# A graph network's hand-over between two layers: four small DMAs against one over 128 partitions

## The chip, the cores and the metric

The kernel runs on one core of one Trainium2 chip. The core has a matrix engine (TensorE, called PE in the profile, with its weight loads as PEld), three engines for elementwise work (VectorE or DVE, ScalarE or ACT, GpSimd or POOL) and a SyncE (SP), which in this kernel only issues transfers. Transfers (DMAs) are issued from SP or from POOL; each engine's instructions and issues start in the order in which they were written. The metric is the device time of one execution in microseconds (us); less is better.

## The reference

The input is a batch of 128 graphs of 128 nodes with 256 features, in float32. Two layers, each a residual step on the normalized input:

```python
# layer 0: all 128 nodes of every graph
h = jnp.maximum(_layernorm(x, axis=-1), 0.0)
x = x + _L0_gnn_ref(h, adj, ...)     # 1x1 and 17-tap convolution, neighbour sums, GRU-like gates
# layer 1: only the nodes in GROUPS, all of them below 25
GROUPS = [list(range(25)), [0, 1, 2, 3, 4, 5, 6, 7, 8], [0, 9, 10, 11, 12, 13, 14],
          [6, 7, 8, 12, 13, 14], [3, 4, 5, 9, 10, 11]]
h = jnp.maximum(_layernorm(x, axis=-1), 0.0)
x = x + _L1_gnn_ref(h, adj, ...)     # five small graph convolutions per graph, fused by weights
return x
```

Layer 1 reads and changes rows 0 to 24 of each graph alone. So rows 32 to 127 are final when layer 0 is done, and the first 32 rows have to be handed over from layer 0 to layer 1.

## The kernel before

Layer 0 works on *groups* of `GB = 4` graphs, 32 groups in all. Its convolution has a first pass (`stage_a`, four batches of 8 groups) and a middle pass per batch (`stage_b`, products in the frequency domain). The neighbour sums and gates follow group by group in `stage_n` and `stage_c`. Layer 1 works on *blocks* of `SB = 16` graphs, that is `QS = 4` groups, 8 blocks in all, in two steps: `prepare` (adjacency, row statistics) and `block` (the convolutions).

Every stage is a Python generator that emits instructions and yields an estimated cost. A small planner (`Order`, `Lane`) takes turns between the generators by those costs and their due times. What it emits is the fixed order of instructions on each engine; at run time the engines only wait for each other through semaphores. Until the last `stage_b` has ended, `stage_n` and `stage_c` run beside `stage_a` and `stage_b`; after it (about 1355 us into the span) they run beside layer 1.

At the end of `stage_c` a group's result stands in the tile `xt`, 128 partitions by 4 rows of 256: partition `32 j + n` holds rows `n`, `n + 32`, `n + 64` and `n + 96` of the group's graph `j` (`WIDE = 32`). `xt` was loaded with the residual input by `load_x` (L358, four DMAs on SP), and L832 (DVE) adds the layer's result. There is one `xt` buffer, so SP's next `load_x` into it waits until all stores out of it have landed, and what stands behind it on SP waits too: the filter weights `wf` (L488), inputs `xa` (L358), the layer's inputs `hT` (L540, L640) and `yt` (L562), and in layer 1 `aj` (L929) and the weights `w` (L897).

The stores are issued from POOL, graph by graph: L838 stores the graph's first 32 rows (`xt[:, 0]`) to a scratch buffer in DRAM, `x1d`, one per block, and L839 stores the other 96 rows to `out`. For the last four groups the block tile of layer 1 exists already; L829 adds straight into it and L838 is left out. POOL's other work, in whose queue the stores stand, is the reciprocal root of the row statistics (L278), the sums `xs` and `wf` of `stage_b` (L496, L497), the gate blend of `stage_c` (L810 to L813), the stores of `hTd`, `yd` and `xmd`, and in layer 1 `b` (L936), `dm` (L962 to L964), `x1h` (L913) and the stores of the finished blocks (L1077).

In layer 1 `load_x1` (L919, on SP, called in `prepare` or `rows_of_x`) fetches a block's hand-over from `x1d` into a tile of 128 partitions by 4 groups by 256. It has two buffers, so it waits for the stores L1077 of the block before the last. `rows_of_x` then computes the row statistics (L275, DVE) and the normalized rows `x1h`. In the trace the block tile is called `x`.

Of the kernel before, what the change touches and what calls it, by code (L numbers as in the profile page):

```python
# [20 lines left out]
GB = 4  # L21
# [10 lines left out]
SB = 16  # L32
QS = SB // GB
# [9 lines left out]
WIDE = 32  # L43
# [165 lines left out]
def kernel(ctx: ExitStack, tc: tile.TileContext, x, adj, consts, vecs, w_se, conv1_w,  # L209
                    conv2_w, w_msg, b_msg, w_ih, w_hh, W1, W2, b2, fusion_w, out):  # L210
    nc = tc.nc
# [15 lines left out]
    x1d = [dr.tile([SB, WIDE, D], FP, name=f"x1d{b}") for b in range(NBLK)]  # L227
# [308 lines left out]
    IN, IN2, X1, N_DONE = {}, {}, {}, set()  # L536
# [119 lines left out]
    def stage_c(q):  # L656
# [108 lines left out]
        xt = LATE["io"].tile([P, 4, D], FP, tag="xt", name=f"xt{q}", bufs=1)  # L765
# [54 lines left out]
        direct = X1.get(q // QS)  # L820
        for h in range(2):
            po = ptmp.tile([P, 2, D], FP, tag="tmp", name=f"po{q}_{h}")
            for i in range(2):
                t = 2 * h + i
# [6 lines left out]
            else:  # L831
                nc.vector.tensor_add(xt[:, 2 * h:2 * h + 2], xt[:, 2 * h:2 * h + 2], po)  # L832
        yield 0.9, 1.5
        for j in range(GB):
            rows = xt[j * WIDE:(j + 1) * WIDE]
            g = q * GB + j
            if direct is None:
                nc.gpsimd.dma_start(out=x1d[g // SB][g % SB], in_=rows[:, 0])  # L838
            nc.gpsimd.dma_start(out=out[g, WIDE:].rearrange("(t n) c -> n t c", n=WIDE),  # L839
                                in_=rows[:, 1:4])  # L840
        C_DONE.add(q)


# [55 lines left out]
    def rows_of_x(blk, wait=True):  # L899

        ready = all(q in C_DONE for q in range(blk * QS, (blk + 1) * QS))
        if blk in S or not (wait or ready and blk - 1 in Y_DONE):
            return
        while not (all(q in C_DONE for q in range(blk * QS, (blk + 1) * QS))
                   and blk - 1 in Y_DONE):
            yield 0.0, 0.5
        if blk not in X1:
            load_x1(blk)
            yield 0.0, 6.0
        pool2 = S["pool2"]  # L910
        x1h = S[blk] = pool2.tile([P, QS, D], FP, tag="x1h", name=f"x1h{blk}", bufs=1)
        normalize(x1h, X1[blk], *moments(X1[blk], "b"))
        nc.gpsimd.tensor_scalar(x1h, x1h, 0.0, None, op0=ALU.max)  # L913
        yield 0.0, 8.0 if wait else 0.0

    def load_x1(blk):
        X1[blk] = S["pool2"].tile([P, QS, D], FP, tag="x1", name=f"x1_{blk}")
        for j in range(GB):
            nc.sync.dma_start(out=X1[blk][j * WIDE:(j + 1) * WIDE],  # L919
                              in_=x1d[blk].rearrange("(q j) n c -> j n q c", j=GB)[j])  # L920

    def prepare(blk):

# [7 lines left out]
        if blk not in X1 and all(q in C_DONE for q in range(blk * QS, (blk + 1) * QS)):  # L931
            load_x1(blk)
# [164 lines left out]
    for blk in range(NBLK):  # L1097
        second += [prepare(blk), block(blk)]
    groups = Lane([stage(q) for q in range(NQ) for stage in (stage_n, stage_c)], ahead=2)
    side = Lane(first, weight=0.5)  # L1100
    order.run(groups, side, until=side)
# [42 lines left out]
```

## Time and profile before

| | us |
|---|---|
| median of 5 runs | 2212.25 (2208.79 to 2215.77) |
| the profiled execution, its own time | 2210.70 |
| its span, first to last instruction | 2208.92 |
| TensorE busy | 2126.2 (96%) |
| VectorE busy | 1161.9 (53%) |
| GpSimd busy | 793.8 (36%) |
| ScalarE busy | 730.4 (33%) |
| 112 stores to `x1d` (L838), time on POOL | 58.4 |
| 128 stores to `out` (L839), time on POOL | 72.0 |
| SP waiting at `load_x` for stores to `out` | 228.6 |

The profile is one execution. A group's line gives the program line, engine, operation, tiles and count. A wait's line reads: who waited (engine, tile, line), for whom, then the total in us, the number of times, and the longest. A DMA's line gives destination and source, the issuing queue, the count, the KB of each and the median time from issue to landing in us. In a timeline a line begins with the start in us and the duration. `PEclk` is the clock that TensorE was granted, as a share of full speed. POOL's DMA issues count as busy time of POOL, SP's do not. Idle time of an engine that is not the bound costs nothing.

### The profile page before, as it was taken

To read this page: it belongs to the slowest core of one execution; us is meant where nothing else is said; L and a number is where in the kernel's file an instruction comes from. 1 tells how busy PE (TensorE), PEld (TensorE's weight loads), DVE (VectorE), ACT (ScalarE), POOL (GpSimd) and SP (SyncE) were. 2 spreads that over 40 slices of the span, in tenths; PEclk is the share of its full clock that TensorE was granted. 3 is DMA by queue.
4 is the path that set the end of the run, shared out by engine and by line. 5 is a ranking of instruction groups with operands and counts; after the bars stand their busy time and mean duration, and the time that the engine had idled before them with its cause. 6 is when DMAs were issued, how large, how long until landed. Compare 5 with 4: busy or idle time off the path is not lost.

```text
span 2208.9 us, 30690 instructions
## 1 busy us (share of the span) xinstructions
PE 2126.2 (96%) x11308; PEld 1676.6 (76%) x11308; DVE 1161.9 (53%) x2659; ACT 730.4 (33%) x1519; POOL 793.8 (36%) x978
## 2 busy tenths in 40 slices
PE   6999899999999999999999999899999999999997
PEld 3578778888878888888788887677777877767765
DVE  4565446645457654446554545554554554454442
ACT  2432233322234432234443332234334333332332
POOL 2227513265523245542225554232223323213320
PEclk9899999999999999999999999999999999999999
DMA  9888624454533354443335444122223223222221
GB/s 182 226 257 266 224 77 128 121 177 148 158 95 99 93 153 148 148 124 87 97 97 155 146 141 140 39 77 69 76 67 87 67 58 87 65 56 61 88 70 48
DMA packets 193976, 259.64 MB, mean 118 GB/s; under 512 B 21981, under 2 KB 157154, under 8 KB 192290
## 3 DMA queue, kind: packets, MB, share of 16 engines
q1 hardware_dynamic: 165682, 175.89, 28.0%
q0 software_dynamic: 27312, 81.03, 12.1%
q8 instruction: 90, 1.47, 0.3%
q10 hardware_dynamic: 832, 0.75, 0.2%
q14 instruction: 60, 0.49, 0.1%
HBM read 178.44 MB, written 79.17 MB: 117 GB/s over the span
## 4 chain that ended last, share of the span: by engine, by line
PE 83%; DVE 8%; DMA 4%; ACT 2%; POOL 2%; issue 1%; SPq 0%; DVEq 0%; POOLq 0%; ACTq 0%
PE p L710 32%; PE pa L502 7%; PE pg L774 5%; PE pc L396 4%; PE pm L592 4%; PE ph L1015 4%; PE pz L1024 4%; PE pb L502 3%; PE pf L409 3%; PE px L617 2%; PE pi L675 2%; PE pc L689 1%; PE ph L383 1%; PE pg L1057 1%; DMA hTd<-hTa 1%
## 5 line engine op out<-in xcount | busy, mean ns | idle before, releaser
L502 PE MATMUL pa<-wf,X 128*128 128x256 f32 x768 | 182.0, 380 | 0.6 <-DMA wf<-wfd 0.6
L278 POOL TENSOR_TENSOR rs<-rs,cst 128x4 f32<-128x4 f32 x40 | 41.4, 1034 | 363.6 <-DVE rs L277 349.8
L502 PEld LDWEIGHTS pa<-wf,X 128*128 128x128 f32 x768 | 144.7, 190 | 23.3 <-issue 3.0
L810 POOL TENSOR_TENSOR d<-hT,r 128x512 f32<-128x512 f32 x64 | 81.9, 1280 | 218.0 <-ACT r L807 218.0
L525 DVE SCALAR_TENSOR_TENSOR y<-pa,kk 128x512 f32<-128x512 f32 x92 | 63.6, 691 | 154.8 <-ACT kk L524 147.4
L496 POOL TENSOR_TENSOR xs<-X 128x256 f32<-128x256 f32 x92 | 68.6, 746 | 190.0 <-PE pb L502 166.8
L710 PE MATMUL p<-th,wrz 128*128 128x256 f32 x512 | 133.9, 384 | 0.0
L710 PE MATMUL p<-tc,wrz 128*128 128x256 f32 x512 | 131.7, 380 | 2.1 <-DVE tc L552 2.1
L710 PE MATMUL p<-tm,wrz 128*128 128x256 f32 x512 | 131.7, 380 | 0.0
L396 PE MATMUL pc<-c1w,hTa 128*128 128x256 f32 x512 | 127.8, 395 | 2.2 <-ACT hTa L385 2.2
L396 PEld LDWEIGHTS pc<-c1w,hTa 128*128 128x128 f32 x512 | 98.4, 196 | 33.0 <-issue 10.3
L592 PE MATMUL pm<-wmsg,hT 128*128 128x256 f32 x512 | 122.7, 384 | 0.0
L774 PE MATMUL pg<-hT,whn 128*128 128x512 f32 x256 | 122.2, 603 | 0.0
L497 POOL TENSOR_TENSOR wf<-wf 128x512 f32<-128x512 f32 x92 | 116.6, 1268 | 11.1 <-DMA wf<-wfd 11.1
L592 PEld LDWEIGHTS pm<-wmsg,hT 128*128 128x128 f32 x512 | 97.0, 192 | 24.4 <-issue 11.3
L1015 PE MATMUL ph<-yz,w 128*128 128x96 f32 (+3 forms) x640 | 111.7, 329 | 2.8 <-DVE yz L1000 1.9
L524 ACT ACTIVATE kk<-pb 128x256 f32<-128x256 f32 x92 | 35.3, 384 | 230.2 <-PE pb L502 230.2
L1017 ACT ACTIVATE hh<-ph,vec 128x96 f32<-128x96 f32 (+3 forms) x160 | 62.7, 402 | 141.6 <-PE ph L1015 134.2
L710 PEld LDWEIGHTS p<-tc,wrz 128*128 128x128 f32 x512 | 96.8, 190 | 16.6 <-DVE tc L552 3.4
L1024 PE MATMUL pz<-hh,w 128*128 128x96 f32 (+3 forms) x640 | 108.1, 323 | 1.3 <-DVE aT L609 1.3
L710 PEld LDWEIGHTS p<-th,wrz 128*128 128x128 f32 x512 | 95.6, 191 | 16.7 <-issue 3.8
L1015 PEld LDWEIGHTS ph<-yz,w 128*128 128x128 f32 x640 | 89.3, 196 | 24.5 <-issue 14.4
(205 smaller groups left out, 4644.6 us busy)
## 6 DMA issues: line engine op xcount, KB each, us to landing
wf<-wfd SPq DMA_DIRECT2D x192, 256.0 KB, 3.2
yd<-y POOLq DMA_DIRECT2D x96, 256.0 KB, 2.5
yt<-yd SPq DMA_DIRECT2D x64, 384.0 KB, 4.2
hT<-hTd SPq DMA_DIRECT2D x40, 512.0 KB, 6.4
w<-in_W SPq DMA_DIRECT2D x40, 512.0 KB, 3.8
xa<-in_x SPq DMA_DIRECT2D x128, 128.0 KB, 4.9
hTd<-hTa POOLq DMA_DIRECT2D x32, 512.0 KB, 4.5
xt<-in_x SPq DMA_DIRECT2D x128, 128.0 KB, 2.8
```

Of the source, the lines that this page charges most:

```text
L396: nc.tensor.matmul(pc[:, i], hT[:, k, (2 * h + i) * N:(2 * h + i + 1) * N], c1w[:, k], start=(k == 0), stop=(k == 1))
L409: nc.tensor.matmul(pf[:, i, :F * NB], h1[:, 2 * h + i, k * P:(k + 1) * P], fwd, start=True, stop=True)
L496: nc.gpsimd.tensor_tensor(XS[f], X[:, :, 2 * f], X[:, :, 2 * f + 1], ALU.add)
L497: nc.gpsimd.tensor_tensor(WF[f][:, :, 2], WF[f][:, :, 0], WF[f][:, :, 1], ALU.add)
L502: nc.tensor.matmul(ps, xk(k), WF[f][:, k, s], start=(k == 0), stop=(k == 1))
L525: nc.vector.scalar_tensor_tensor(y, pa, 2.0, kk[:, None].to_broadcast([P, 2, D]), op0=ALU.mult, op1=ALU.subtract)
L592: nc.tensor.matmul(pm[:, i], hT[:, k, j * N:(j + 1) * N], wmsg[:, k], start=(k == 0), stop=(k == 1))
L710: nc.tensor.matmul(ps[:, m], w[:, i, k, m * P:(m + 1) * P], factor(i, x, t), start=first and j == 0, stop=last and j == len(n) - 1)
L774: nc.tensor.matmul(pg, whn[:, k, dc * P:(dc + 1) * P], hT[:, k], start=(k == 0), stop=(k == 1))
L810: nc.gpsimd.tensor_sub(d, hT[:, dc], r[:, dc])
L1015: nc.tensor.matmul(ph, w1[:, k, m * P:(m + 1) * P], yz[:, k, :, o:o + n], start=(k == 0), stop=(k == 1))
L1024: nc.tensor.matmul(pz, w2[:, g, m, cc * P:(cc + 1) * P], hs[g][:, m], start=(m == 0), stop=(m == 3))
```

## The change

The four stores of a group's first 32 rows become one store over all 128 partitions, placed ahead of the four stores to `out`. In layer 1 the four loads of a block's rows, one per graph position `j`, become one load over all 128 partitions. The bytes, the DRAM buffer and the order of all other instructions stay.

```diff
         yield 0.9, 1.5
+        if direct is None:
+            b0 = q % QS * GB
+            nc.gpsimd.dma_start(out=x1d[q // QS][b0:b0 + GB].rearrange("b n c -> (b n) c"),
+                                in_=xt[:, 0])
         for j in range(GB):
-            rows = xt[j * WIDE:(j + 1) * WIDE]
-            g = q * GB + j
-            if direct is None:
-                nc.gpsimd.dma_start(out=x1d[g // SB][g % SB], in_=rows[:, 0])
-            nc.gpsimd.dma_start(out=out[g, WIDE:].rearrange("(t n) c -> n t c", n=WIDE),
-                                in_=rows[:, 1:4])
+            nc.gpsimd.dma_start(out=out[q * GB + j, WIDE:].rearrange("(t n) c -> n t c", n=WIDE),
+                                in_=xt[j * WIDE:(j + 1) * WIDE, 1:4])
         C_DONE.add(q)
...
     def load_x1(blk):
         X1[blk] = S["pool2"].tile([P, QS, D], FP, tag="x1", name=f"x1_{blk}")
-        for j in range(GB):
-            nc.sync.dma_start(out=X1[blk][j * WIDE:(j + 1) * WIDE],
-                              in_=x1d[blk].rearrange("(q j) n c -> j n q c", j=GB)[j])
+        nc.sync.dma_start(out=X1[blk],
+                          in_=x1d[blk].rearrange("(q j) n c -> (j n) q c", j=GB))
```

## The prediction

> **What bounds the kernel now.** I read the page first, for which engine is busy, then the busy time by stretches, because the edited transfers begin at 335.6 us and the loads of layer 1 at 1356.9 us, then what TensorE (PE) waits for in each stretch, and last the edited transfers themselves.
>
> From the page, and from the stretches (us, then per engine the busy time and instructions; PEclk is the granted clock):
>
> ```profile
> PE 2126.2 (96%) x11308; PEld 1676.6 (76%) x11308; DVE 1161.9 (53%) x2659; ACT 730.4 (33%) x1519; POOL 793.8 (36%) x978
> ...
> 330.00:1355.00 1025.00, 1019.35 (x5185) 840.72 (x5186) 569.31 (x1257) 345.04 (x702) 430.61 (x518) 1.00 0.43 129
> 1355.00:2209.00 854.00, 810.51 (x4492) 617.91 (x4488) 423.88 (x1005) 280.69 (x597) 240.49 (x302) 0.98 0.25 70
> ```
>
> PE is the bound. Between 330 and 1355 it is idle for 1025.00 - 1019.35 = 5.65 us, at full clock. Only the stretch from 1355 on has room: 43.5 us idle, and a clock of 0.98. What PE waited for there, longest first, and the only wait for POOL (GpSimd) before 1355:
>
> ```profile
> PE pc L689 <- ACT xi L677: 12.0, 6, 3.2
> PE pg L974 <- DVE dd L969: 6.7, 4, 4.7
> PE po L826 <- POOL z L813: 3.6, 2, 2.8
> ...
> PE po L826 <- POOL z L813: 0.2, 1, 0.2
> ```
>
> The reader is to see what is missing: no row in which PE waits for `x1d`, for the block rows `x` or for an `xt` transfer. The edited transfers:
>
> ```profile
> out<-xt POOLq DMA_DIRECT2D x128, 96.0 KB, 2.2
> x1d<-xt POOLq DMA_DIRECT2D x112, 32.0 KB, 1.9
> x<-x1d SPq DMA_DIRECT2D x28, 128.0 KB, 2.7
> ...
> L838 POOL DMA_DIRECT2D x1d<-xt x112: 503/513/644, 335.6 to 1839.7; - x112
> L919 SPq DMA_DIRECT2D x<-x1d x28: 302/425/4844, 1356.9 to 2078.1; - x28
> ```
>
> So an issue holds POOL for about half a microsecond, whatever it carries, and the stores go out alternating (POOL's timeline at one group):
>
> ```profile
> 1836.45 0.52 POOL L838 DMA_DIRECT2D x1d<-xt  x1 [1.27 <-DVE xt L832]
> 1837.05 0.55 POOL L839 DMA_DIRECT2D out<-xt  x1
> ...
> 1840.22 0.55 POOL L839 DMA_DIRECT2D out<-xt  x1
> 1840.79 3.39 POOL L936 TENSOR_TENSOR b<-aj,cst 25x400 f32<-25x400 f32 x8
> ```
>
> **The change, part by part.**
>
> *Stores, removed and added.* 28 groups store to `x1d` (112 / 4). Removed: 112 issues of 0.521 us (58.4 us on POOL by the groups of instructions). Added: 28 issues over 128 partitions. No such store is in the trace; the bounds are 0.513 us (32 rows of 1 KB) and 0.591 us (`hTd<-hTa`, 128 rows of 4 KB); nearest is `yd<-y`, 128 partitions of 2 KB, with 0.564 us. I take that: 15.8 us. POOL is relieved of 42.6 us, 1.52 us per group. On the path: POOL can only hand this on where its next instruction follows the stores at once. In POOL's timeline that is so after 10 of the 28 groups (after 339.4, 490.4, 537.4, 584.3, 627.0, 738.3, 861.5, 915.9, 1264.0 and 1840.2); after the other 18 POOL idles from 1.0 us (1207.4) to 37.5 us (1786.1). Nine of the ten lie before 1355, where PE waits for POOL 0.2 us in all. The tenth brings `b` (L936) forward, whose reader (L941, DVE) starts at 1859.7, 15 us after it is done. Taken: -0.2 us. Bounds: 0, and 10 x 1.52 = -15.2 us if nothing covered it, which PE's idle time cuts to -5.65 us.
>
> *Stores, moved.* The rows of graphs 1 to 3 and the last three `out` stores move forward in POOL's queue. The last `out` issue began 3.77 us after the first store (1836.45 to 1840.22); now 0.56 + 3 x 0.56 = 2.2 us. With 2.2 us to landing, `xt` is free about 1.5 us earlier. SP holds its next `xt` load for just that (L358 waits 228.6 us for `out<-xt` in SP's waits), and everything queued behind it on SP moves up by as much: `wf`, `xa`, `w` and `aj` loads. PE waits for DMA after 330 us in no row, so this is worth 0; the bound is again the 5.65 us. The 128 KB store itself should land between 1.9 us (32 KB) and 4.5 us (`hTd<-hTa`, 512 KB); at 4.5 us it is still no later than the last `out`.
>
> *Wait added.* The one store waits for all four `xt` loads, where each piece waited for its own, and for DVE's add. Behind it stand four `out` stores and POOL's next work. The loads are old by then: at 1381.3 us they are issued, at 1451.9 us DVE adds into `xt`. 0 us; with the cover gone, at most a load's landing, 2.8 us by its row.
>
> *Loads of layer 1.* Removed: 28 issues, added 7. SP saves 21 x 0.425 = 8.9 us, and bounds nothing. A 512 KB load with rows of 1 KB is not in the trace. Below: 2.7 us (the quarter). Above: 6.4 us (`hT<-hTd`, 512 KB). Nearest in form is `yt<-yd` (96 partitions, 4 rows of 1 KB), 4.2 us for 384 KB; scaled by bytes an estimate of 5.6 us. Before, the last quarter landed about 1.75 + 2.7 = 4.4 us after the first issue, now 0.4 + 5.6 = 6.0 us: 1.6 us later (bounds -1.3 and +2.4). The cover is the distance to the first statistics (L275, DVE):
>
> ```profile
> 2076.78 1.75 SPq L919 DMA_DIRECT2D x<-x1d  x4
> ...
> 2094.52 0.42 DVE L275 BATCH_NORM_STATS2 st<-x 128x6 f32<-128x256 f32 x1
> ```
>
> That is block 6, the tightest: landed at 2081.2, used at 2094.5, 13.3 us of slack. The other six have 24 us (block 0, 1363.2 to 1390.2) to 63 us. So 0 us. Without cover: 7 x 2.4 = 16.8 us.
>
> *Clock.* PE's clock is the one thing a small shift can tip. The rows of two places, each with the idle stretch first:
>
> ```profile
> 1355.00:1361.00 6.00, 2.94 (x14) 1.00 1.11 267
> 1361.00:1372.00 11.00, 10.87 (x40) 0.69 0.55 133
> ...
> 1440.00:1454.00 14.00, 11.34 (x53) 0.88 0.41 124
> 1454.00:1458.00 4.00, 4.00 (x21) 1.00 0.56 126
> ```
>
> After a gap of 3.19 us the clock is down to 0.69 for 11 us, a loss of 3.4 us. In the second pair a gap of 2.66 us (at 1443.2) stands with 0.12 x 14 = 1.7 us lost. From 1355 on 0.02 x 854 = 17 us go that way. Shifts of a microsecond can take one such loss away or add one; I take 0, with +-1.7 us a piece. The Trainium skill, "TensorE: Matmul & The Clock Gate", section "HAM oscillation", names idle gaps of more than about 3.4 us as those that throttle; the rows here show the loss after shorter ones too. By the page one new gap of 3.2 us would cost an estimated 3.2 us, by the rows 6.6.
>
> *The sum.* -0.2 (stores) + 0 (moves) + 0 (wait) + 0 (loads) + 0 (clock) = -0.2 us against the profiled execution, 2210.7 us (span 2208.9 and 1.8 around it). The median of the runs, 2212.25, is 1.55 us above that, so 2212.0 us on the median's scale.
>
> A rule that would make it far better: the Trainium skill, "DMA: Bandwidth & Descriptors", sections "Anatomy of one DMA" and "Rules for kernel authors", puts about 2.0 us of fixed cost on each DMA and advises one 128-partition transfer in place of disjoint partition parts. By it 105 fewer DMAs would be an estimated 210 us in a kernel that waited for each. The trace has them issued 0.5 us apart with 1.9 us each to landing, overlapped and unawaited: 0 us.
>
> **Rivals.**
>
> 1. *POOL's relief reaches PE.* For it: ten groups without a pause on POOL, and PE does wait for POOL's `z`, 3.6 us after 1355. Against: neither of those two waits (1900.0 and 2062.6) has a store shortly ahead; POOL was held by `x1h` (L913). At the most all idle time before 1355, both waits and one clock loss: 5.65 + 3.6 + 1.7 = 11 us, 2201 us.
>
> 2. *Slower: POOL's work slides next to DVE's.* POOL's next operation starts 1.5 us earlier and may now run beside DVE's two-input sums. At 1355 to 1359, beside POOL's L810 to L813, the sums L552 to L554 took 1.37 to 1.48 us instead of 0.42, and PE's 3.19 us gap at 1358 followed: 3.2 + 3.4 us of clock = 6.6 us per occurrence; 2219 us with one, 2225 with two. One is enough to count as slower. Against: nine of the ten groups that can slide lie where slow sums (1264.8: 2.17 us; 832.6: 1.33 us) left PE no gap.
>
> 3. *The one load lands late.* It must be over 13 us late to reach block 6 and 24 us for block 0; the longest landing of a quarter was 5.9 us. If the cover failed everywhere, 16.8 us: 2229 us.
>
> 4. *The change does not do what it says*: the one DMA costs POOL as much as four, 0.5 us for each 32 rows. Against: 128-row stores have 0.56 to 0.59 us. Then all stays: 2212 us.
>
> **How the numbers follow.** A measurement of this kernel can tell about 0.2% (4.4 us) from no change: the five runs span 7.0 us. Nothing happens that PE sees: 0.45, own range 2207 to 2217 (three clock losses either way), of which 0.04 fall to faster and 0.03 to slower. Rival 1: 0.24, faster. Rival 2: 0.20, slower. Rival 3: 0.06, slower. Rival 4: 0.05, same. Faster 0.04 + 0.24 = 0.28; same 0.38 + 0.05 = 0.43; slower 0.03 + 0.20 + 0.06 = 0.29. The range goes from rival 1's bound, 2201, to between one and two occurrences of rival 2, 2223; rival 3 and the rest of rival 2, some 0.12, are left out.
>
> **What would show it.** Right: `x1d<-xt` x28 at 0.55 to 0.6 us, 128 KB; `x<-x1d` x7, 512 KB, landing in 4 to 7 us; POOL busy near 751 us; PE's idle time from 330 to 1355 between 4 and 7 us, and its waits after 1355 with the same names and sizes within a microsecond. Wrong: a row of PE or DVE waiting for `x<-x1d`; new sums of over 1 us beside POOL with a PE gap behind them; the 12.0 us at L689 or the 6.7 us at L974 clearly smaller or larger; a granted clock from 1355 on that leaves 0.98.

## The result, and the profile after

The kernel with the one store and the one load takes **2220.53 us** (median of 43 runs, 2203.52 to 2236.87). The kernel before, in 80 runs, has 2213.51 us (2194.74 to 2225.47). The ratio is 1.0029 with a 95% interval of 1.0017 to 1.0040: 6.4 us slower, with 3.8 to 8.9 us possible. The forecast was no change that can be told (2212.0 us). It was wrong.

Runs of one kernel lie up to 33 us apart, because PE is granted another mean clock in each. The execution of after that was profiled is the shortest of its runs: a span of 2201.7 us at a mean clock of 0.988, where that of before has 2208.9 us at 0.984. So the two spans can't be subtracted from each other. What can be compared is stretches without a dip of the clock, and single waits.

First the page of after (busy time of each engine and number of instructions):

```profile
PE 2115.8 (96%) x11308; PEld 1669.7 (76%) x11308; DVE 1167.8 (53%) x2659; ACT 730.3 (33%) x1519; POOL 750.5 (34%) x894
```

POOL's relief came as worked out: 793.8 - 750.5 = 43.3 us (42.6 were forecast). DVE, which the change doesn't touch, is 5.9 us busier here with the same 2659 instructions; but the second traces of both kernels have 1163.2 us (before) and 1164.6 us (after), so most of the 5.9 us is scatter between executions.

The edited transfers, in the table of DMA issues of after (last number: median us to landing):

```profile
out<-xt POOLq DMA_DIRECT2D x128, 96.0 KB, 2.4
...
x1d<-xt POOLq DMA_DIRECT2D x28, 128.0 KB, 2.1
x<-x1d SPq DMA_DIRECT2D x7, 512.0 KB
```

and the new store in the view of its own line (shortest, median and longest issue in ns):

```profile
L836 POOL DMA_DIRECT2D x1d<-xt x28: 542/588/652, 328.3 to 1826.8; - x28
```

Next the stretches. After had reached the change of stages (`L689`) 5.8 us earlier than before, so its stretches are cut at 1348 instead of 1355 us (columns: length, then busy time and instructions of PE, PEld, DVE, ACT and POOL, the granted clock, DMA share, GB/s):

```profile
330.00:1348.00 1018.00, 1011.14 (x5139) 833.63 (x5137) 564.81 (x1243) 340.96 (x694) 397.95 (x456) 1.00 0.43 129
1348.00:2201.70 853.70, 806.78 (x4496) 614.36 (x4494) 425.73 (x1008) 281.60 (x598) 227.12 (x275) 0.98 0.24 70
```

In the first one PE is idle for 1018.00 - 1011.14 = 6.86 us, where before has 5.65: 1.2 us more, at full clock. PE's waits up to 1348 us, in the view of waits of after (total, times, longest), put a name to it. Before has the first of these rows with 1.5 us, 2 times, and the others unchanged:

```profile
PE p L710 <- DVE tc L552: 2.7, 3, 1.3
PE ph L383 <- DVE aT L609: 1.1, 1, 1.1
PE ph L383 <- DVE xa L283: 1.0, 2, 0.8
...
PE po L826 <- POOL z L813: 0.2, 1, 0.2
```

The waits of after from 1348 us on are those that the prediction shows of before, with one exception:

```profile
PE pc L689 <- ACT xi L677: 12.0, 6, 3.2
PE pg L973 <- DVE dd L968: 6.7, 4, 4.7
PE po L826 <- POOL z L813: 4.1, 3, 2.8
```

There is one more wait for `z`, of 0.4 us. It doesn't belong to the change: the kernel before_last_sp below, with the old stores, has the same row (4.1 us, 3 times), and stores_only, with the new ones, has 3.6 us, 2 times, as before. No wait for a transfer is new.

**The new gap.** In the timeline of after, the new wait stands at one place (start, duration, engine, and in brackets the idle time and who ended it):

```profile
1252.98 0.54 POOL L836 DMA_DIRECT2D x1d<-xt  x1 [0.94 <-DVE xt L832]
1253.57 2.22 POOL L839 DMA_DIRECT2D out<-xt  x4
...
1255.81 0.73 POOL L496 TENSOR_TENSOR xs<-X 128x256 f32<-128x256 f32 x1
1255.82 2.23 DVE L551 TENSOR_TENSOR tc<-xc 128x256 f32<-128x256 f32 x1
...
1256.49 1.26 POOL L497 TENSOR_TENSOR wf<-wf 128x512 f32<-128x512 f32 x1
...
1258.08 0.42 DVE L552 TENSOR_TENSOR tc<-xc,tc 128x256 f32<-128x256 f32 x1
...
1258.56 1.13 PE L710 MATMUL p<-tc,wrz 128*128 128x256 f32 x4 [1.21 <-DVE tc L552]
```

In the timeline of before, at the same group, the stores end later, and POOL's `xs` and `wf` meet other sums:

```profile
1263.12 0.42 DVE L551 TENSOR_TENSOR tc<-xc 128x256 f32<-128x256 f32 x1
...
1263.57 0.43 DVE L552 TENSOR_TENSOR tc<-xc,tc 128x256 f32<-128x256 f32 x1
...
1263.91 0.95 DVE L553 TENSOR_TENSOR tc<-xc 128x256 f32<-128x256 f32 x1
1264.03 0.56 POOL L839 DMA_DIRECT2D out<-xt  x1
...
1264.48 1.03 PE L710 MATMUL p<-tc,wrz 128*128 128x256 f32 x4
1264.60 0.84 POOL L496 TENSOR_TENSOR xs<-X 128x256 f32<-128x256 f32 x1
1264.78 2.17 DVE L554 TENSOR_TENSOR tc<-tc,xc 128x256 f32<-128x256 f32 x1
...
1265.41 1.25 POOL L497 TENSOR_TENSOR wf<-wf 128x512 f32<-128x512 f32 x1
```

Both kernels have a sum of 2.2 us that goes on until 0.3 us after `wf` has ended (1258.05 and 1257.75; 1266.95 and 1266.66). In before it is the last of the four, L554, whose result PE needs later. In after it is the first, and the other three stand behind it. PE waits 1.21 us for L552.

What the gap costs can be measured between two events of PE that both kernels have, with no dip of the clock between them. In the timeline of PE, before:

```profile
1101.20 0.48 PE L396 MATMUL pc<-c1w,hTa 128*128 128x256 f32 x1 [0.32 <-ACT hTa L385]
...
1361.13 0.55 PE L689 MATMUL pc<-cst,xi 128*128 128x128 f32 x3 [3.19 <-ACT xi L677]
```

and after:

```profile
1093.91 0.48 PE L396 MATMUL pc<-c1w,hTa 128*128 128x256 f32 x1 [0.32 <-ACT hTa L385]
...
1355.32 0.54 PE L689 MATMUL pc<-cst,xi 128*128 128x128 f32 x2 [3.20 <-ACT xi L677]
```

That is 259.93 us before and 261.41 us after: **+1.5 us**. It is called the *stretch* below.

**The end.** The last work of the program is DVE's add L1068 (L1067 in after). It ends at 2197.94 + 0.42 = 2198.36 in before. Then POOL issues four stores. In the timelines of the end, before:

```profile
2197.94 0.42 DVE L1068 TENSOR_TENSOR x<-x,pfu 128x256 f32<-128x256 f32 x1 [1.09 <-PE pfu L1066]
2198.66 2.18 POOL L1077 DMA_DIRECT2D out<-x  x4 [35.85 <-DVE x L1068]
```

and after:

```profile
2187.78 0.42 DVE L1067 TENSOR_TENSOR x<-x,pfu 128x256 f32<-128x256 f32 x1 [1.09 <-PE pfu L1065]
2188.50 2.18 POOL L1076 DMA_DIRECT2D out<-x  x4 [35.85 <-DVE x L1067]
```

Then comes POOL's closing DRAIN. It stands in the view of the kernel's last line (durations in ns: shortest, median, longest of three; then the first and the last start). Before:

```profile
L1140 POOLq DRAIN  x3: 46/169/7756, 2200.0 to 2208.7; - x3
```

After:

```profile
L1139 POOLq DRAIN  x3: 46/102/11022, 2189.9 to 2201.4; - x3
```

The longest DRAIN grew from 7.76 to 11.02 us. No engine computes beside it. The stretches of before at its middle and of the whole tail, and the whole tail of after (columns as above), show that data moves only at its start:

```profile
2203.00:2206.00 3.00, 0.00 (x0) 0.00 (x0) 0.00 (x0) 0.00 (x0) 0.00 (x0) 0.50 0.00 0
2198.36:2208.92 10.56, 0.00 (x0) 0.00 (x0) 0.00 (x1) 0.00 (x0) 2.18 (x4) 0.65 0.21 50
...
2188.20:2201.68 13.48, 0.00 (x0) 0.00 (x0) 0.01 (x1) 0.00 (x0) 2.18 (x4) 0.63 0.16 40
```

From the end of the last add to the end of the span it is 2208.92 - 2198.36 = 10.6 us in before and 2201.68 - 2188.20 = 13.5 us in after: **+2.9 us**. This is called the *tail* below. The granted clock falls to 0.50 in it, which matters further down.

### The profile page after: what moved, and what is told of

The parts are those of the page before. It is cut to its first block, busy times and chain, and to the rows that moved or that the text cites. A ratio compares the mean times of both kernels' runs of the same rounds, so it can differ in the third digit from the quotient of the medians.

```text
span 2201.7 us, 30482 instructions
## 1 busy us (share of the span) xinstructions
PE 2115.8 (96%) x11308; PEld 1669.7 (76%) x11308; DVE 1167.8 (53%) x2659; ACT 730.3 (33%) x1519; POOL 750.5 (34%) x894
## 3 DMA queue, kind: packets, MB, share of 16 engines
q0 software_dynamic: 25072, 81.03, 11.9%
## 4 chain that ended last, share of the span: by engine, by line
PE 82%; DVE 8%; POOL 2%; DMA 2%; ACT 2%; issue 2%; SPq 0%; DVEq 0%; POOLq 0%; ACTq 0%
PE p L710 32%; PE pa L502 7%; PE pg L774 5%; PE pc L396 4%; PE pz L1023 4%; PE ph L1014 4%; PE pm L592 4%; PE pb L502 3%; PE pf L409 3%; PE px L617 2%; PE pi L675 2%; PE ph L383 1%; PE pc L689 1%; PE po L826 1%; PE pg L1056 1%
## 5 line engine op out<-in xcount | busy, mean ns | idle before, releaser
L710 PEld LDWEIGHTS p<-tm,wrz 128*128 128x128 f32 x512 | 97.3, 190 | 13.2
```

What stands on the lines that cost most here:

```text
L710: nc.tensor.matmul(ps[:, m], w[:, i, k, m * P:(m + 1) * P], factor(i, x, t), start=first and j == 0, stop=last and j == len(n) - 1)
```

## The experiments

The table has what the traces and times of all kernels gave; "transfers" is the number of DMAs that POOL issues, and a ratio is against runs of before on the same chip.

| kernel | POOL's transfers | longest DRAIN | tail | stretch | median us | ratio to before, 95% |
|---|---|---|---|---|---|---|
| before | 447 | 7.76 | 10.6 | 259.93 | 2213.51 | |
| after | 363 | 11.02 | 13.5 | 261.41 | 2220.53 | 1.0029 [1.0017, 1.0040] |
| again_before | 447 | 7.75 | 10.6 | 259.92 | 2214.69 | 1.0006 [0.9985, 1.0028] |
| again_after | 363 | 11.01 | 13.5 | 261.40 | 2219.95 | 1.0034 [1.0013, 1.0055] |
| stores_only | 363 | 11.02 | 13.5 | 261.39 | 2218.35 | 1.0022 [1.0000, 1.0044] |
| load_only | 447 | 7.74 | 10.2 | 259.93 | 2214.60 | 1.0002 [0.9984, 1.0019] |
| q17_old | 366 | 11.26 | 13.7 | 259.91 | 2214.97 | 1.0006 [0.9987, 1.0026] |
| pieces_ahead | 447 | 7.75 | 10.6 | 259.92 | 2218.78 (one run) | |
| before_last_sp | 443 | 7.36 | 5.1 | 259.92 | 2208.19 | 0.9986 [0.9970, 1.0002] |
| after_last_sp | 359 | 10.78 | 4.7 | 261.38 | 2212.31 | 0.9991 [0.9968, 1.0014] |
| halves | 391 | 4.10 | 6.5 | 261.47 | 2222.99 (one run) | |
| after_q17_last_sp | 362 | 11.03 | 5.0 | 259.91 | 2206.52 | 0.9962 [0.9937, 0.9986] |
| before_last_two | 443 | 7.36 | 5.2 | 259.90 | 2207.20 | 0.9966 [0.9943, 0.9990] |
| halves_q17_old | 393 | 4.38 | 6.8 | 259.90 | 2213.44 | 0.9989 [0.9967, 1.0011] |

The intervals of the times are 3 to 5 us wide on each side. The stretch and the tail repeat to 0.1 us for the same kernel, so the mechanisms are read from them, and the times only say whether the sum agrees. In all ten kernels that issue their last stores from POOL, the tail is the longest DRAIN plus 2.4 to 2.8 us, from 6.5 us with a DRAIN of 4.10 to 13.7 us with one of 11.26.

**Is it there, and in which part?** Both kernels once more, unchanged, and each half of the change alone. The expectations call the theories C (the clock of the runs), W (more work or waiting on PE's path), P (POOL's work slides next to DVE's sums) and L (the one load).

> The kernel before, unchanged, for a second trace and for the scatter of the comparison. Every theory: ratio 1.000, with an interval that shows what one such comparison can tell. Theory C (the clock): span times mean granted clock is the same within 0.1% in every run, near 2173 us, as in the trace of before (2208.9 x 0.9837 = 2172.8), and the runs differ by the clock alone.

> The changed kernel, unchanged. Its first profiled run was its fastest (2203.5 against a median of 2220.5), so a trace of a usual run is wanted. Theory C (the clock): span times clock stays near 2174 us, 1 to 2 us above before, and the rest of the 6 us is more time at half clock, in stretches of 3.4 us; ratio 1.002 to 1.004. Theory W (work): the rest is idle time of TensorE that the fast run did not have, at waits with new names, and span times clock is about 6 us above before.

stores_only has the change of the stores, load_only that of the loads:

```diff
-            if direct is None:
-                nc.gpsimd.dma_start(out=x1d[g // SB][g % SB], in_=rows[:, 0])
...
+        if direct is None:
+            b0 = q % QS * GB
+            nc.gpsimd.dma_start(out=x1d[q // QS][b0:b0 + GB].rearrange("b n c -> (b n) c"),
+                                in_=xt[:, 0])
```

```diff
-        for j in range(GB):
-            nc.sync.dma_start(out=X1[blk][j * WIDE:(j + 1) * WIDE],
-                              in_=x1d[blk].rearrange("(q j) n c -> j n q c", j=GB)[j])
+        nc.sync.dma_start(out=X1[blk],
+                          in_=x1d[blk].rearrange("(q j) n c -> (j n) q c", j=GB))
```

> Only the stores as in the changed kernel (one over 128 partitions), the loads of layer 1 as before (four a block). Theory P (POOL's work slides next to DVE's sums): the whole loss is here, ratio 1.002 to 1.004, and the trace has the new 1.2 us gap of TensorE at L710 behind a slow L551 near 1258 us. Theory L (the one load): 1.000 within 0.0015, and the gap at 1258 us costs nothing that can be told.

> Only the load as in the changed kernel (one a block), the stores as before (four a group). Theory P: 1.000 within 0.0015, no gap of TensorE at 1258 us. Theory L: ratio 1.002 to 1.004, with the difference after 1355 us.

The loss repeats: 1.0034 for after, 1.0006 for before. The stores alone have it, with the same stretch (261.39) and the same DRAIN (11.02); the one load has neither, and 1.0002. So the load is free, as forecast, and the loss belongs to the stores.

How much of it is the clock is seen in the line through each version's runs, span against mean granted clock. At 0.982 it gives 2211.6 us for before (35 runs, +-0.4) and 2215.3 us for after (44 runs, +-0.4), so 3.7 us stay at equal clock; with all 104 runs of before that stand beside the experiments (2212.2) it is 3.1 us.

But the mean clock contains the tail, where PE stands still and its clock falls to 0.50: by the rows of the tail above it loses 10.56 x 0.35 = 3.7 us of full clock in before and 13.48 x 0.37 = 5.0 us in after. So 1.3 us of the longer tail count as clock in this comparison, and at equal clock during the work the loss is an estimated 4.4 to 5.0 us. The rest of the 6.4 us goes with a lower clock during the work (the mean over the whole span is 0.9806 in the 44 runs of after and 0.9821 in the 35 of before). The clock differs so much from run to run that this rest, 1.4 to 2 us, is uncertain by some 1.3 us; whether the change causes it stays open. Neither theory C (span times clock 1 to 2 us higher) nor W (about 6 us) was right as written: it is 3.3 us higher, 2175.1 against 2171.8.

**Take the gap away.** One group, the one of the timelines above, goes back to the old stores; the other 27 keep the new one.

q17_old, against after:

```diff
+        if q == 17:
+            for j in range(GB):
+                rows = xt[j * WIDE:(j + 1) * WIDE]
+                g = q * GB + j
+                if direct is None:
+                    nc.gpsimd.dma_start(out=x1d[g // SB][g % SB], in_=rows[:, 0])
+                nc.gpsimd.dma_start(out=out[g, WIDE:].rearrange("(t n) c -> n t c", n=WIDE),
+                                    in_=rows[:, 1:4])
+        else:
...
```

> The kernel after, but one group, the eighteenth (q = 17, the one whose stores end at 1255.8 us in the profile after), stored in the old way, with four 32-row stores between its four stores to out. Theory G (the 1.2 us gap of PE at L710 comes from this one group: its stores end 1.5 us earlier, so POOL's xs and wf run beside DVE's L551 to L554): the row 'PE p L710 <- DVE tc L552' falls from 3 waits with 1.3 us the longest to the 2 of before, PE's work from L396 (about 1100) to L689 (about 1361) takes 259.9 us of full clock again instead of 261.4, and the time falls by 1.2 to 1.5 us against after: about 2218.5 us, ratio 1.0022 to before. Theory D (POOL's closing DRAIN is what is left of the loss): the DRAIN stays at 11.0 us, for POOL still issues 81 of the 84 stores fewer. A theory of the clock alone (C): the gap stays or goes with no effect on the time, ratio 1.003.

The stretch is back at 259.91 us. In the timeline of this kernel the slow sum is again the last of the four, and PE does not wait:

```profile
1266.51 0.42 DVE L551 TENSOR_TENSOR tc<-xc 128x256 f32<-128x256 f32 x1
...
1267.97 0.86 POOL L496 TENSOR_TENSOR xs<-X 128x256 f32<-128x256 f32 x1
1268.17 2.17 DVE L554 TENSOR_TENSOR tc<-tc,xc 128x256 f32<-128x256 f32 x1
```

So theory G holds: all of the 1.5 us comes from this one group. The time fell further than the trace explains (1.0006, where 1.0022 was expected), but its interval reaches to 1.0026. The DRAIN did *not* stay: with 3 transfers more it took 11.26 us instead of 11.02. That is against the simple reading, that fewer transfers make it longer.

**Hide the DRAIN.** The last block's four stores are issued by SP, so that POOL has issued its last transfer 38 us earlier (2162.8 instead of 2200.8 us in the profile of before).

The same edit in before_last_sp and after_last_sp:

```diff
-            nc.gpsimd.dma_start(
+            (nc.sync if blk == NBLK - 1 else nc.gpsimd).dma_start(
                 out=out[blk * SB:(blk + 1) * SB, :WIDE].rearrange("(q j) n c -> j n q c", j=GB)[j],
```

> The kernel before, with the four stores of the last block's rows issued by SP instead of POOL. POOL's last issue is then that of block 6 (2160.5 us), and its closing DRAIN can run beside the rest of layer 1. Theory D (the DRAIN is on the path, 7.75 us of it in before): it starts near 2162.8 and ends before PE does (2197.9); what is left at the end is four issues on SP (0.3 to 0.4 us each) and one landing of 2.6 to 3 us, so the end comes about 5 to 6 us after the last add (2198.4) instead of 10.5: 4 to 5.5 us faster, ratio 0.9975 to 0.998. If the DRAIN only waits for the last stores to land, it moves to wherever these end, and the time stays within 1 us: ratio 1.000.

> The kernel after, with the same edit. Theory D: the 11.0 us DRAIN is hidden as well, so it gains 7.5 to 9 us on after (3 us more than before gains), and stands only 2 to 3 us above before_last_sp: about 2211.5 us, ratio 0.9985 to 1.000 to before. What is left between the two is the gap of theory G (1.2 to 1.5 us) and up to 1 us in layer 1. Theory C, and any theory without the DRAIN: the distance between the two versions stays at 6 us, so 2219 to 2220 us if the edit is worth nothing, and 6 us above before_last_sp in any case.

The last stores in SP's timeline of before_last_sp:

```profile
2204.50 1.79 SPq L1077 DMA_DIRECT2D out<-x  x4
```

Its DRAIN, in the view of the last line:

```profile
L1140 POOLq DRAIN  x3: 46/102/7357, 2168.2 to 2209.0; - x3
```

and in after_last_sp:

```profile
L1139 POOLq DRAIN  x3: 46/102/10782, 2153.3 to 2194.2; - x3
```

The DRAIN now starts at 2168.2 and 2153.3 us and is over long before PE is. The tails are 5.1 and 4.7 us, nearly the same for both kernels: with the DRAIN hidden, the 2.9 us between them are gone. The tail of before_last_sp is 5.5 us shorter than that of before. Of this the times show 2.7 us (0.9986, interval from -6.6 to +0.4 us), and for after_last_sp some 2 us below before, where the tail and the gap make 10.6 - 4.7 - 1.5 = 4.4 us. Both agree within their intervals and prove little alone.

**What sets the DRAIN's length?** Order and number of the stores were changed together, so one kernel changes the order alone, and one the number.

pieces_ahead, against before:

```diff
         for j in range(GB):
-            rows = xt[j * WIDE:(j + 1) * WIDE]
-            g = q * GB + j
             if direct is None:
-                nc.gpsimd.dma_start(out=x1d[g // SB][g % SB], in_=rows[:, 0])
-            nc.gpsimd.dma_start(out=out[g, WIDE:].rearrange("(t n) c -> n t c", n=WIDE),
-                                in_=rows[:, 1:4])
+                g = q * GB + j
+                nc.gpsimd.dma_start(out=x1d[g // SB][g % SB], in_=xt[j * WIDE:(j + 1) * WIDE, 0])
+        for j in range(GB):
+            nc.gpsimd.dma_start(out=out[q * GB + j, WIDE:].rearrange("(t n) c -> n t c", n=WIDE),
+                                in_=xt[j * WIDE:(j + 1) * WIDE, 1:4])
```

halves, against after:

```diff
         if direct is None:
-            b0 = q % QS * GB
-            nc.gpsimd.dma_start(out=x1d[q // QS][b0:b0 + GB].rearrange("b n c -> (b n) c"),
-                                in_=xt[:, 0])
+            for j in (0, 2):
+                b0 = q % QS * GB + j
+                nc.gpsimd.dma_start(out=x1d[q // QS][b0:b0 + 2].rearrange("b n c -> (b n) c"),
+                                    in_=xt[j * WIDE:(j + 2) * WIDE, 0])
```

> The kernel before, with the order of the stores changed but not their number: a group's four 32-row stores to x1d first, then its four stores to out. If the closing DRAIN follows the number of POOL's stores, it stays at 7.75 us; if it follows their order or what stands last in the queue, it is 11.0 us as in after. The gap at L710 (theory G) stays away, since POOL is free no earlier than before: longest wait there 0.4 to 1.3 us with 2 waits, L396 to L689 259.9 us at full clock.

> The kernel after, with two stores of 64 partitions per group in place of the one of 128: POOL issues 391 transfers, where after has 363, the version with one old group 366, before 447. The closing DRAIN took 11.02 us with 363, 11.26 with 366, 10.78 with 359; 7.75 with 447 and 7.36 with 443. Theory R (the DRAIN pays for the transfers that came since something like a ring was last folded back: it rises by 0.06 to 0.10 us for each, and falls back somewhere between 366 and 443): with 391 the DRAIN is shorter than the 7.36 us, 2 to 4 us, unless the fall lies above 391, then 13 us. Theory N (the fewer transfers, the longer, evenly: 3.27 us over 84): 9.9 us. Theory B (7.75 us with the old pieces, 11 us without): 11 us. POOL's stores of a group end 1.0 us earlier than in before, so the gap at L710 may come in part: 0 to 1.2 us.

With the order alone changed the DRAIN stays at 7.75 us. With 391 transfers it is shorter than in either kernel, in the view of the last line of halves:

```profile
L1140 POOLq DRAIN  x3: 46/102/4097, 2216.3 to 2220.9; - x3
```

That is near theory R's 2 to 4 us, and it rules out N (9.9 us) and B (11 us). In order of the number of transfers, 359, 362, 363, 366, 391, 393, 443 and 447, the DRAIN takes 10.78, 11.03, 11.02, 11.26, 4.10, 4.38, 7.36 and 7.76 us: a saw-tooth, that rises by 0.06 to 0.14 us for a transfer, except from 362 to 363, where it stays, and falls back between 366 and 391. Nothing here shows what folds back. It is no even count of the transfers, and not of the packets of POOL's queue either, which are 24960 with 362 transfers and 25072 with 363.

The gap came back in full in halves (stretch 261.47), where 0 to 1.2 us were expected. A group's stores end earlier than in before by less than in after, and now it is the second of the four sums that meets `xs` and `wf`:

```profile
1271.58 0.81 POOL L496 TENSOR_TENSOR xs<-X 128x256 f32<-128x256 f32 x1
...
1271.85 2.06 DVE L552 TENSOR_TENSOR tc<-xc,tc 128x256 f32<-128x256 f32 x1
1272.37 1.25 POOL L497 TENSOR_TENSOR wf<-wf 128x512 f32<-128x512 f32 x1
...
1273.96 1.13 PE L710 MATMUL p<-tc,wrz 128*128 128x256 f32 x4 [1.28 <-DVE tc L552]
```

**Take both causes away.** after_q17_last_sp is q17_old with the edit of after_last_sp: the one group in the old way, and the last stores on SP. before_last_two is before with its last stores on two queues:

```diff
-            nc.gpsimd.dma_start(
+            eng = (nc.sync, nc.scalar)[j % 2] if blk == NBLK - 1 else nc.gpsimd
+            eng.dma_start(
```

> The kernel after with both causes taken away: the one group in the old way, and the last block's stores issued by SP. If the gap (1.5 us) and the DRAIN (2.9 us in the tail) are the loss, nothing is left but the under 1 us of layer 1: L396 to L689 259.9 us at full clock, tail after the last add 4.7 to 5.1 us, and the time within 1 us of the version of before with the last stores on SP, 2208 us where before is at 2211 to 2213: ratio 0.9975 to 0.9990. A theory in which something else of the change costs: 2 us or more above that version, ratio 0.9995 or more.

> The kernel before with the last block's four stores issued two by SP and two by ScalarE, so that POOL's closing DRAIN runs beside the work before. With all four on SP the tail after the last add was 5.07 us instead of 10.56. Two issues of 0.43 us less in a row: tail 4.2 us, 6.3 us less than before, ratio 0.9970 to 0.9980 (the version with all four on SP had 0.9986 [0.9970, 1.0002], where its tail alone would have made 0.9975). If hiding the DRAIN is not worth what the tail shows, 0.9985 or more.

Without gap and DRAIN, nothing of the loss is left: stretch 259.91, tail 5.0, ratio 0.9962 [0.9937, 0.9986]. The rival, a third cost of 2 us or more, would have had 0.9995 or more. Its 12 runs had a higher mean clock (0.984) than those of before beside it (0.982), though. At 0.982 their line gives 2210.2 +-1.8 us, that of before_last_sp 2208.3 +-0.6; so the traces show no third cost, and the times don't exclude one of up to 2 us. The kernel beats before and after, and so does before_last_two, 0.9966 [0.9943, 0.9990]; the two can't be told apart. The second queue itself brought nothing: the tail is 5.2 us, not the 4.2 expected, so issuing isn't what the tail waits for. Its ratio is better than its tail explains (10.56 - 5.23 = 5.3 us less of 2213 is 0.9976); its runs had a mean clock of 0.985, those of before beside it 0.982.

**A short DRAIN on POOL.** Last, a version with 393 transfers and all stores of the last block from POOL as in before. halves_q17_old, against q17_old:

```diff
         else:
             if direct is None:
-                b0 = q % QS * GB
-                nc.gpsimd.dma_start(out=x1d[q // QS][b0:b0 + GB].rearrange("b n c -> (b n) c"),
-                                    in_=xt[:, 0])
+                for j in (0, 2):
+                    b0 = q % QS * GB + j
+                    nc.gpsimd.dma_start(out=x1d[q // QS][b0:b0 + 2].rearrange("b n c -> (b n) c"),
+                                        in_=xt[j * WIDE:(j + 2) * WIDE, 0])
```

> The kernel after, with two stores of 64 partitions per group, and the one group q = 17 in the old way; POOL issues 393 transfers, all last stores from POOL as in before. Theory R (the closing DRAIN follows POOL's transfers since the last fold, 4.10 us with 391): 4.1 to 4.4 us, so a tail of 6.5 to 6.9 us after the last add where before has 10.56 and after 13.46; the gap at L710 stays away (L396 to L689 259.9 us at full clock); with 0 to 1 us for layer 1 the time is 3 to 4 us below before, ratio 0.9982 to 0.9987, and 9 to 10 us below after. A theory in which the DRAIN's length is only a record and another wait would end the program: ratio 1.000 to 1.003.

Its DRAIN, in the view of the last line:

```profile
L1149 POOLq DRAIN  x3: 46/102/4376, 2210.4 to 2215.3; - x3
```

The DRAIN was forecast at 4.1 to 4.4 us and took 4.38; the tail 6.8 (6.5 to 6.9), the stretch 259.90. The ratio, 0.9989 [0.9967, 1.0011], holds the expected 0.9982 to 0.9987 but does not exclude 1.000. The rival, that the DRAIN is only a record, falls by the tail, which is 3.7 us shorter than in before, and not by the time.

## Why the prediction was wrong

**The step that failed is the sum.** It lists stores, moves, wait, loads and clock, and ends with the last instruction of the program's work. The end of the program has no term in it, though the prediction removed 84 of POOL's transfers, and POOL's closing DRAIN was there to be read in the trace of before, with 7756 ns, on the path and with nothing beside it. A bound was to be had from that row: the DRAIN could have become 7.8 us shorter at most, and how much longer no row said. It made +2.9 us in the tail, the largest part of the loss.

**The second term is the path of "Stores, removed and added".** POOL's relief was costed by POOL's rows among PE's waits (0.2 us before 1355), and so at -0.2 us. But POOL reaches PE through DVE too: POOL's earlier `xs` and `wf` slow DVE's sums, and PE waits for "DVE tc". That is rival 2 as written, at one place. It was given 0.20, and priced at 6.6 us with the clock; it cost 1.5 us, because the gap was 1.2 us instead of 3.2 and the granted clock stayed at 1.00. Its "against" was misread: the slow sum at 1264.8 us left no gap because the *last* of the four was caught (and that at 832.6 was the first, but took only 1.33 us); the 1.5 us by which POOL came earlier were enough to catch the first, for 2.23 us.

The Trainium skill, "SBUF — State Buffer", section "Who interferes with whom", says that a VectorE instruction with two inputs in SBUF contends with a GpSimd instruction that reads SBUF, and calls this an exclusive lock. The rows agree: whichever sum meets `xs` and `wf` ends 0.3 us after `wf`, with 2.06 to 2.23 us in place of 0.42. So the question for rival 2 was which sum would be caught, and not whether sums had been slow before.

The two terms make 1.5 + 2.9 = 4.4 us of the 6.4 measured, inside its interval (3.8 to 8.9). They agree with the 4.4 to 5.0 us that stay at equal clock during the work. The other 2.0 us go with the lower clock of these runs; no row shows their cause, and it stays open.

**What held.** The stores cost what was said (0.588 us each where 0.564 was taken; 128 KB land in 2.1 us, between the bounds of 1.9 and 4.5). *Moves*: PE waits no longer for any transfer than before. *Wait added*: none of the stores waits for a load of `xt`; 22 of 28 wait for DVE's add. *Loads*: free, by load_only; the landing of the 512 KB load is not in the records, so the 4 to 7 us stay unseen. *Clock*: 1.00 up to 1348 us and 0.98 behind in the profiled execution, as in before; over all runs the mean was lower than before's, as said above. *Rival 1* did not come: PE's waits for POOL did not become shorter (4.1 us from 1348 on, where before has 3.6). *Rival 3* and *rival 4* are excluded by load_only and by the 0.588 us.

## What to carry to other kernels

End the sum at the last instruction of the trace, and not at the last work: after its last add this kernel spends 10.6 us, and who issues the last stores, and how many came before on that engine, is worth 3 to 9 us there. If GpSimd issues many transfers, let another queue issue the last ones, so that its closing DRAIN runs beside other work. And an engine that gets free time early is not only a relief: look which two-input sums of VectorE its next operation will meet, and which of them is needed first.

## What the runs showed of the hardware

- POOL's closing DRAIN takes 4.1 to 11.3 us, repeats within 15 ns for the same program, and is no even function of the work: 28 transfers more (391 for 363) made it 6.9 us shorter, 84 more (447) 3.3 us shorter.
- The DRAIN is about as long if it is started some 41 us before the end (7.36 us with 443 transfers, 10.78 with 359), and then costs nothing.
- A sum of VectorE that takes 0.42 us alone takes 2.1 to 2.2 us if it meets two operations of GpSimd, `xs` and `wf`; a shift of 1.5 us decided whether PE noticed it.
